# Four PSUM banks as one tile, paired clips and exponentials, and a third set of exponentials added on VectorE

## The chip, the cores and the metric

The kernel runs on one core of a Trainium2 chip. The metric is the device time of one execution in microseconds (us). The times come from repeated runs; the profile is of one further execution, in which the hardware profiler recorded every instruction. In the text PE is TensorE, DVE is VectorE, ACT is ScalarE, POOL is GpSimd and SP is SyncE, which here issues loads.

## The reference, cut to what matters

Eight batches of 112 tokens with 512 channels go through two layers. Each layer is a cross-attention over 375 context rows followed by a feed-forward network, each on a layer-normalised input and added to the residual. The change touches the second cross-attention, which has 16 heads of 32 channels:

```python
scores = jnp.einsum('bhsd,bhtd->bhst', q, k) / scale
scores = jnp.clip(scores, -50.0, 50.0)
scores = jnp.where(attend, scores, -10000.0)
scores = jnp.clip(scores, -50.0, 50.0)
probs = jax.nn.softmax(scores, axis=-1)
ctx = jnp.einsum('bhst,bhtd->bhsd', probs, v)
ctx = ctx.transpose(0, 2, 1, 3).reshape(B, S, H)
delta = rs * (ctx @ Wo.T + bo)
delta = (delta - mu) / jnp.sqrt(var + EPS_LN) * ln_gamma + ln_beta
x = x + delta
```

Since scores are clipped to 50 in size, the kernel takes no maximum: it clips, takes the exponential, and divides the weighted sum of values by the sum of the exponentials.

## The kernel before

The kernel is one long program. Layer 0 (attention, then a feed-forward network with ternary weights) fills the first 206 us of the span; then come the queries of layer 1; then, from 234.6 to 395.6 us, the second attention, called the stage below; then the last feed-forward network.

In the stage the loop runs over batches `b` (0 to 7) and, in each, over three chunks `c` of 125 context rows. The order in which each engine gets its work is the order in which the program writes it: `manual_schedule` covers all five engines here. Each engine works strictly through its own queue, so an instruction that waits holds up everything behind it on that engine.

For each chunk:

- `scores(b, c)`: PE multiplies keys with queries, for 4 groups `dc` of four heads `r` each. The four heads of a group lie on four different row quarters of PE, run side by side, and write four different PSUM banks, one per `r`. Each bank holds 4 x 112 = 448 columns. DVE then clips each bank into SBUF (L910, with `upper` carrying the mask) and ACT takes the exponential in place (L911). The results are `sets[(b + c) % 3][r]`.
- `fill(1)`: one step of a generator that projects keys (L194, four steps per batch) or values (L203, three steps) of a later batch. It keeps PE occupied while DVE and ACT work on the chunk. Its result goes through one of two PSUM buffers called "mm", which ACT copies out (L197 or L205). The table `STEPS` says in how many chunks of a batch a step is taken; batch 4 has two, all the others three.
- `sums` of the chunk before: PE multiplies exponentials with values (`num`, L931). With the last chunk of a batch it also forms the denominator (`den`, L926), by multiplying the exponentials with a block of ones. The exponentials of chunks 0 and 1 have by then been added together by `add(b)` (L897, on POOL in batches 0 to 6, on DVE in batch 7), so `den` takes two passes: the added set, and chunk 2. ACT copies both out (L937, L938).

Beside this each batch carries work for others:

- chunk 0: DVE finishes a transpose of earlier tokens (L848), then `project_end(b - 3)` (L822 to L827), which waits for POOL's `f` and tokens (L815, L816).
- chunk 1: `divide(b - 1)` on DVE: reciprocals of the denominators (L947) and products (L948).
- chunk 2: `write4(b - 3)` on DVE (L837), `project_product(b - 2)` on PE (L803, into an "mm" buffer, from the divided attention), then `project_begin(b - 2)`: DVE adds the bias out of that buffer (L809), takes moments and a scaled difference (L143 to L817), POOL takes an inverse root step by step (L105 to L109) and updates tokens (L816). Then PE transposes what `write4` wrote (L844, into the other "mm" buffer).

In most chunks POOL and ACT also convert integer weights of the last feed-forward network (L880 on ACT, L882 on POOL), out of two buffers `raw` that SP refills by DMA (L869) as soon as L882 has read them. `convert_integers` stands ahead of `scores` in each chunk, `add(b)` ahead of it at chunk 2.

The PSUM tiles named "s" come from the pool `ps_s`, with four buffers of one bank each. The query stage before (L742, L225) and the last feed-forward network (L1039, L1040) take theirs from it too.

Of the kernel before, what the change touches and what calls it, by code (L numbers as in the profile page):

```python
# [23 lines left out]
F32 = mybir.dt.float32  # L24
# [6 lines left out]
ALU = mybir.AluOpType  # L31
AX = mybir.AxisListType
PSUM = bass.MemoryType.PSUM
ENGINES = mybir.EngineType

P = 128
B, T, D = 8, 112, 512
KC = D // P
S2, CK = 375, 125
NCK = S2 // CK  # L40
# [5 lines left out]
NR = P // HD  # L46
# [10 lines left out]
CLIP = 50.0 / SC1  # L57
# [7 lines left out]

SPLIT = 2.0 ** -12
LESS = 1.0 - 2.0 ** -13


@with_exitstack  # L70
def two_layers(ctx: ExitStack, tc: tile.TileContext, x, ctxT, ctxN, mask0, mask1, w1, w2, w3,
               wq, wk, wv, wo, bq, bk, bv, bo, gamma, beta, rscale,
               wg, sg, wu, su, wd, sd, out):
    nc = tc.nc
# [630 lines left out]

    tailp = ctx.enter_context(tc.tile_pool(name="tailp", bufs=1, side="right"))

    ps_s = ctx.enter_context(tc.tile_pool(name="ps_s1", bufs=4, space=PSUM))
    ps_mm = ctx.enter_context(tc.tile_pool(name="ps_mm1", bufs=2, space=PSUM))
    kv_psum[0] = ps_mm  # L710

# [11 lines left out]
    upper = tailp.tile([CK, NCK, B], F32, name="upper")  # L723
# [127 lines left out]
    with tc.tile_pool(name="work2", bufs=1, side="right") as work2, \  # L851
            tc.tile_pool(name="ps_av", bufs=1, space=PSUM) as ps_av, \
            tc.manual_schedule(engines={ENGINES.PE, ENGINES.SP, ENGINES.DVE,
                                        ENGINES.Activation, ENGINES.Pool}):

        todo = [(w, which, half, c, min(PIECE, HALVES[which][half + 1] - c))
                for which, w in enumerate((wg, wu, wd)) for half in range(2)
                for c in range(HALVES[which][half], HALVES[which][half + 1], PIECE)]  # L860
        due = {(0, 1): 2, (0, 2): 2, (1, 0): 1, (1, 1): 2, (1, 2): 2, (2, 0): 1,
               (3, 1): 2, (3, 2): 2, (4, 0): 1, (5, 1): 2, (5, 2): 2, (6, 0): 1,
               (6, 1): 2, (6, 2): 2, (7, 0): 1, (7, 1): 2, (7, 2): 2}
        loaded = []

        def load_integers(count):
            for w, which, half, c, n in todo[:count]:
                raw = work2.tile([P, PIECE], I32, name="raw", bufs=2)[:, :n]
                nc.sync.dma_start(out=raw, in_=w[:, c:c + n])  # L869
                loaded.append((raw, which, half, c - HALVES[which][half], n))  # L870
            del todo[:count]

        def convert_integers():
            for raw, which, half, c, n in loaded:
                if (which, half) not in halves:
                    halves[which, half] = slab("w", F32R)
                t = halves[which, half][:, c:c + n]

                k = pieces.pop()
                nc.scalar.activation(t, raw, AF.Square, bias=zero_point,  # L880
                                     accum_out=squares[:, k:k + 1])
                nc.gpsimd.tensor_scalar(t, raw, -128.0, 1.0, ALU.add, ALU.mult)  # L882
            loaded.clear()

        sets = [[work2.tile([P, KC, T], F32, name=f"e{i}{r}") for r in range(NR)]  # L890
                for i in range(NCK)]

        def add(b):
            add = (nc.gpsimd if b in ADD_POOL else nc.vector).tensor_add
            for r in range(NR):
                e, e1 = (sets[(b + c) % NCK][r][:CK] for c in range(2))
                add(e, e, e1)  # L897

        def scores(b, c):
            kT = kvs_of[b][0]  # L900
            ss = [ps_s.tile([CK, KC, T], F32, name="s") for r in range(NR)]
            for dc in range(KC):
                for r in range(NR):
                    rows = slice(r * HD, (r + 1) * HD)
                    nc.tensor.matmul(ss[r][:, dc, :], lhsT=kT[rows, dc, c * CK:(c + 1) * CK],  # L905
                                     rhs=qT[rows, dc, b * T:(b + 1) * T], start=True, stop=True)
            es = sets[(b + c) % NCK]
            for r in range(NR):
                e = es[r][:CK]
                nc.vector.tensor_scalar(e, ss[r], upper[:, c, b:b + 1], -CLIP, ALU.min, ALU.max)  # L910
                nc.scalar.activation(e, e, AF.Exp, scale=SC1)  # L911
            return es

        def sums(b, c, es):
            if c == 0:
                sums.num = ps_av.tile([P, KC, T], F32, name="num")
            num = sums.num
            v = kvs_of[b][1]  # L920
            if c == NCK - 1:
                den = ps_av.tile([P, KC, T], F32, name="den")
                added = sets[b % NCK]
                for k, of in enumerate((added, es)):
                    for r in range(NR):
                        nc.tensor.matmul(den[r * HD:(r + 1) * HD], lhsT=ones[:CK, :HD],  # L926
                                         rhs=of[r][:CK], start=(k == 0), stop=(k == 1))
            for dc in range(KC):
                for r in range(NR):
                    head = slice((4 * dc + r) * HD, (4 * dc + r + 1) * HD)  # L930
                    nc.tensor.matmul(num[r * HD:(r + 1) * HD, dc, :], lhsT=v[:, c, head],  # L931
                                     rhs=es[r][:CK, dc, :], start=(c == 0 and dc == 0),
                                     stop=(c == NCK - 1 and dc == KC - 1))
            if c == NCK - 1:

                rden = added[0]
                nc.scalar.copy(rden, den)  # L937
                nc.scalar.copy(qT[:, :, b * T:(b + 1) * T], num)  # L938
                rdens[b] = rden

        def divide(b):

            n = (b + 1) * T - (b + 1) * T // P * P
            for t0, t1 in ((0, T - n), (T - n, T)):
                rden, of = rdens[b][:, :, t0:t1], qT[:, :, b * T + t0:b * T + t1]
                if t1 > t0:
                    nc.vector.reciprocal(rden, rden)  # L947
                    nc.vector.tensor_mul(of, of, rden)  # L948


        STEPS = [3, 3, 3, 3, 2, 3, 3, 3]
        ADD_POOL = range(B - 1)
        last, rdens, later = None, {}, []
        folding = fold_bias()
        counts = list(due.values())
        load_integers(counts.pop(0))
        for b in range(B):
            for c in range(NCK):
                if c == 2 and b in ADD_POOL:
                    add(b)  # L960
                if (b, c) in due:
                    convert_integers()
                    if counts:
                        load_integers(counts.pop(0))
                es = scores(b, c)
                if c == 2 and b not in ADD_POOL:
                    add(b)
                if c < STEPS[b]:
                    fill(1)
                if c == NCK - 1:  # L970
                    sums(*last)
                if (b, c) == (B - 1, NCK - 1):
                    over = tailp.tile([P, 29], F32, name="over")
                    nc.gpsimd.tensor_scalar(over, squares, WIDE, 1.0, ALU.is_gt, ALU.mult)
                if b == 0 and c > 0:
                    next(folding)
                if c == 0:
                    while later:
                        later.pop()()
                    if b >= 3:  # L980
                        project_end(b - 3)
                elif c == 1 and b >= 1:
                    divide(b - 1)
                elif c == 2:
                    turned = 3 <= b < 3 + GROUPS[0][1]
                    if turned:
                        write4(b - 3)
                    if b >= 2:
                        project_product(b - 2)
                    if b == B - 1:  # L990

                        hits = ps_s.tile([1, 29], F32, name="s")
                        nc.tensor.matmul(hits, lhsT=ones[:, :1], rhs=over, start=True, stop=True)
                        wide = tailp.tile([1, 1], I32, name="wide")
                        nc.vector.tensor_reduce(wide, hits, AX.X, ALU.max)
                    if b >= 2:
                        project_begin(b - 2)
                    if turned:
                        later.append(transpose4(b - 3, ps_mm, "mm"))
                if last and c < NCK - 1:  # L1000
                    sums(*last)
                last = b, c, es

        nc.scalar.activation(stat.tile([CK, 1], F32, name="peak")[:], es[-1][:CK, 0, :1], AF.Silu)
        sums(*last)
        divide(B - 1)
        project_end(B - 3)
# [197 lines left out]
```

## Time and profile before

| | |
|---|---|
| runs | 516.91, 517.08, 518.55 us; median 517.08 |
| profiled execution | 516.34 us, its span 514.2 us, mean granted PE clock 0.997 |
| second attention stage | 234.6 to 395.6 us of the span |
| PE start of the chunks (b, 0) for b = 4, 5, 6, 7 | 310.77, 329.15, 350.62, 370.95 us |
| clips L910 | 96 of 125 x 448, mean 677 ns |
| exponentials L911 | 96 of 125 x 448, mean 570 ns |
| adds L897 on POOL | 28 of 125 x 448, mean 1213 ns |
| denominators L926 | 128 rows of 125 x 448 columns, 16 per batch, in some 1.5 us |

The span runs from the first to the last instruction; the time of an execution has some 2 us around it. In timeline rows the columns are the start, the duration of the merged rows, engine, line, operation, output and inputs with their shapes, the number of instructions, and in brackets how long the engine stood idle before and what released it. A float32 matrix product shows as two rows, so the 8 products of a denominator show as 16 rows. Rows that follow each other on one engine overlap a little; the distance from start to start tells what one costs in a series.

### The profile page before, as it was taken

How to read it: one execution, taken by the hardware profiler on the slowest of the kernel's cores; microseconds unless marked ns; L12 is line 12 of the kernel's file. 1: busy time of each engine (PE TensorE's matmuls, PEld its weight loads, DVE VectorE, ACT ScalarE, POOL GpSimd, SP SyncE). 2: the span in 40 equal slices, each digit the busy share in tenths (PEclk: the TensorE clock that was granted, in tenths of full speed). 3: DMA queues.
4: the chain of work that ended last, by engine and by line, in shares of the span. 5: the costliest groups of instructions: out<-in, count | busy, mean ns of one | idle time of the engine just before them, and what ended most of it. 6: DMA issues, size and time to landing. Idle time of an engine off the chain costs nothing.

```text
span 514.2 us, 8868 instructions
## 1 busy us (share of the span) xinstructions
PE 502.5 (98%) x3402; PEld 315.8 (61%) x3402; DVE 337.2 (66%) x815; ACT 252.8 (49%) x438; POOL 134.4 (26%) x221
## 2 busy tenths in 40 slices
PE   9999999999999999999999999999999999999995
PEld 6445554455545455696565565555555788889984
DVE  3552548767798987965676688986897753334432
ACT  0326656857565666236675366465665233103310
POOL 0000121110111064211551475674754430000000
PEclk9999999999999999999999999999999999999998
DMA  8998795200120100122421112012320000010001
GB/s 241 347 407 326 268 324 205 80 18 0 61 82 1 60 2 0 45 101 61 162 68 51 62 52 62 3 53 62 98 69 13 20 1 1 20 42 20 1 20 48
DMA packets 13489, 45.77 MB, mean 89 GB/s; under 512 B 2097, under 2 KB 3392, under 8 KB 12288
## 3 DMA queue, kind: packets, MB, share of 16 engines
q1 hardware_dynamic: 11888, 41.43, 23.5%
q0 software_dynamic: 1248, 3.70, 2.2%
q8 instruction: 29, 0.48, 0.4%
q14 instruction: 20, 0.16, 0.1%
q10 hardware_dynamic: 304, 0.01, 0.0%
HBM read 41.46 MB, written 1.84 MB: 84 GB/s over the span
## 4 chain that ended last, share of the span: by engine, by line
PE 47%; DVE 6%; POOL 2%; ACT 1%; DMA 1%; issue 1%; DVEq 0%; POOLq 0%; ACTq 0%
PE s L1045 14%; PE mm L203 8%; PE down L1067 7%; PE mm L803 3%; PE s L905 3%; PE num L931 2%; PE mm L194 2%; DVE e L910 2%; PE den L926 2%; PE mm L740 1%; PE mm L738 1%; DMA raw<-in_wd_dram 1%; PE s L744 1%; DVE e L947 1%; ACT e L911 1%
## 5 line engine op out<-in xcount | busy, mean ns | idle before, releaser
L203 PE MATMUL mm<-wv,cT 128*125 128x512 f32 x192 | 87.6, 599 | 0.0
L194 PE MATMUL mm<-cT,wk 128*128 128x375 f32 x256 | 87.3, 485 | 0.0
L1045 PE MATMUL s<-h4T,w 128*128 128x512 f32 (+1 forms) x352 | 72.6, 367 | 0.2 <-PE num L931 0.2
L1045 PEld LDWEIGHTS s<-h4T,w 128*128 128x128 f32 x352 | 63.5, 188 | 8.8 <-PE num L931 0.4
L910 DVE TENSOR_SCALAR e<-s,upper 125x448 f32<-125x448 f32 x96 | 59.0, 677 | 14.7 <-PE s L905 13.9
L911 ACT ACTIVATE e<-e 125x448 f32<-125x448 f32 x96 | 51.6, 570 | 27.8 <-DVE e L910 27.3
L194 PEld LDWEIGHTS mm<-cT,wk 128*128 128x128 f32 x256 | 46.8, 190 | 27.6 <-issue 1.0
L203 PEld LDWEIGHTS mm<-wv,cT 128*125 128x125 f32 x192 | 34.5, 187 | 38.0 <-issue 36.4
L897 POOL TENSOR_TENSOR e<-e,e 125x448 f32<-125x448 f32 x28 | 33.1, 1213 | 15.8 <-PE num L931 15.8
L1067 PE MATMUL down<-w,gu 128*128 128x512 f32 (+1 forms) x176 | 37.0, 367 | 0.0
L541 PE MATMUL mm<-w_q,q_qT 128*128 128x512 fp8e4 (+1 forms) x168 | 34.8, 361 | 0.8 <-DVE tokens L583 0.4
L439 POOL DMA_DIRECT2D tokens<-x x14 | 10.7, 768 | 90.3 <-DVE x L433 63.0
L1067 PEld LDWEIGHTS down<-w,gu 128*128 128x128 f32 x176 | 29.8, 188 | 5.7
L880 ACT ACTIVATE w<-raw,zero_point 128x640 fp32r<-128x640 int32 (+2 forms) x29 | 22.6, 781 | 20.4 <-DMA raw<-in_wd_dram 9.2
L1053 ACT CAST gu<-gu 128x512 fp32r<-128x512 f32 (+1 forms) x22 | 12.5, 568 | 39.6 <-DVE gu L1051 39.6
L570 POOL TENSOR_SCALAR q<-gu 128x704 bf16<-128x704 f32 x14 | 10.8, 790 | 79.8 <-ACT gu L567 79.8
L882 POOL TENSOR_SCALAR w<-raw 128x640 fp32r<-128x640 int32 (+2 forms) x29 | 20.7, 724 | 36.0 <-ACT w L880 35.8
L905 PE MATMUL s<-qT,kv 32*125 32x112 f32 x768 | 29.4, 280 | 0.6 <-DVE qT L748 0.3
L1051 DVE SCALAR_TENSOR_TENSOR gu<-s,su,gu 128x512 f32<-128x512 f32 (+1 forms) x22 | 15.1, 684 | 21.8 <-PE s L1045 20.6
L905 PEld LDWEIGHTS s<-qT,kv 32*125 32x125 f32 x768 | 24.5, 183 | 7.1 <-issue 5.8
L541 PEld LDWEIGHTS <-q_qT 128*128 128x128 bf16 x168 | 16.3, 98 | 19.7 <-issue 2.5
L931 PEld LDWEIGHTS num<-e,kv 125*32 125x32 f32 x768 | 18.4, 110 | 13.6 <-issue 7.9
(238 smaller groups left out, 798.6 us busy)
## 6 DMA issues: line engine op xcount, KB each, us to landing
cT<-in_ctxT_dram SPq DMA_DIRECT2D x13, 750.0 KB, 6.1
raw<-in_w_dram SPq DMA_DIRECT2D x6, 1408.0 KB, 20.3
cN<-in_ctxN_dram SPq DMA_DIRECT2D x8, 768.0 KB, 4.5
raw<-in_wg_dram SPq DMA_DIRECT2D x8, 320.0 KB, 3.0
raw<-in_wu_dram SPq DMA_DIRECT2D x8, 320.0 KB, 2.9
raw<-in_wd_dram SPq DMA_DIRECT2D x8, 320.0 KB, 3.1
out_dram<-d SPq DMA_DIRECT2D x6, 256.0 KB, 2.0
wk<-in_wk_dram SPq DMA_DIRECT2D x4, 256.0 KB, 4.9
```

The source lines that it names most:

```text
L194: nc.tensor.matmul(ps[dc], lhsT=wk_s[:, kc, dc * P:(dc + 1) * P], rhs=cT[:, kc, :], start=(kc == 0), stop=(kc == KC - 1))
L203: nc.tensor.matmul(ps, lhsT=cT[:, kc, c * CK:(c + 1) * CK], rhs=wv_s[:, kc, :], start=(kc == 0), stop=(kc == KC - 1))
L541: nc.tensor.matmul(ps[:, :n], lhsT=qT[:, kc, :], rhs=w[:, kc * H + n0:kc * H + n0 + n], start=(kc == 0), stop=(kc == KC - 1))
L880: nc.scalar.activation(t, raw, AF.Square, bias=zero_point, accum_out=squares[:, k:k + 1])
L882: nc.gpsimd.tensor_scalar(t, raw, -128.0, 1.0, ALU.add, ALU.mult)
L897: add(e, e, e1)
L905: nc.tensor.matmul(ss[r][:, dc, :], lhsT=kT[rows, dc, c * CK:(c + 1) * CK], rhs=qT[rows, dc, b * T:(b + 1) * T], start=True, stop=True)
L910: nc.vector.tensor_scalar(e, ss[r], upper[:, c, b:b + 1], -CLIP, ALU.min, ALU.max)
L911: nc.scalar.activation(e, e, AF.Exp, scale=SC1)
L931: nc.tensor.matmul(num[r * HD:(r + 1) * HD, dc, :], lhsT=v[:, c, head], rhs=es[r][:CK, dc, :], start=(c == 0 and dc == 0), stop=(c == NCK ...
L1045: nc.tensor.matmul(ps[:, :n], lhsT=w[:, c:c + P], rhs=h4T[k][:, kc, :n], start=(kc == 0 and k == 0), stop=(kc == KC - 1 and k == 1))
L1067: nc.tensor.matmul(ps, lhsT=gus[k][:, hc, j * P:(j + 1) * P], rhs=w[:, c + n0:c + n0 + n], start=(hc == 0 and k == 0), stop=(hc == HC - 1 ...
```

## The change

Three things change.

The pool `ps_s` gets a single tile of four banks, and a small class `Banks` hands out parts of it: `tile` gives the next bank, in rotation, and `pair` gives two neighbouring banks, starting at an even one.

In the stage, `scores` takes two pairs in place of four tiles. Heads 0 and 1 are in the first pair and heads 2 and 3 in the second. One clip and one exponential then treat 2 x 448 elements per partition. The exponentials lie in tiles for two heads (`twos`); `add(b)` adds two heads' groups at a time.

In batches 2 to 6 (`ADD_LAST`), DVE adds the exponentials of chunk 2 to the sum that POOL has made of chunks 0 and 1. The two adds stand in chunk 2 behind `write4` and `project_product` and ahead of `project_begin`. The denominator of these batches is then one pass over the sum.

```diff
+class Banks:
+    def __init__(self, pool):
+        self.all = pool.tile([P, 4, 512], F32, name="s")
+        self.next = 0
+    def tile(self, shape, dtype, name):
+        n = 1
+        for d in shape[1:]:
+            n *= d
+        t = self.all[:shape[0], self.next, :n]
+        self.next = (self.next + 1) % 4
+        return t if len(shape) == 2 else t.rearrange("p (a b) -> p a b", a=shape[1])
+    def pair(self):
+        k = (self.next + 1) // 2 * 2 % 4
+        self.next = (k + 2) % 4
+        return self.all[:, k:k + 2, :]
...
-    ps_s = ctx.enter_context(tc.tile_pool(name="ps_s1", bufs=4, space=PSUM))
+    ps_s = Banks(ctx.enter_context(tc.tile_pool(name="ps_s1", bufs=1, space=PSUM)))
...
-        sets = [[work2.tile([P, KC, T], F32, name=f"e{i}{r}") for r in range(NR)]
+        twos = [[work2.tile([P, 2, KC, T], F32, name=f"e{i}{h}") for h in range(NR // 2)]
                 for i in range(NCK)]
+        sets = [[two[r // 2][:, r % 2] for r in range(NR)] for two in twos]
...
-            for r in range(NR):
-                e, e1 = (sets[(b + c) % NCK][r][:CK] for c in range(2))
+            for h in range(NR // 2):
+                e, e1 = (twos[(b + c) % NCK][h][:CK] for c in range(2))
                 add(e, e, e1)
+        def add_last(b):
+            for h in range(NR // 2):
+                e, e1 = (twos[(b + c) % NCK][h][:CK] for c in (0, NCK - 1))
+                nc.vector.tensor_add(e, e, e1)
...
-            ss = [ps_s.tile([CK, KC, T], F32, name="s") for r in range(NR)]
+            ss = [ps_s.pair() for h in range(NR // 2)]
...
-                    nc.tensor.matmul(ss[r][:, dc, :], lhsT=kT[rows, dc, c * CK:(c + 1) * CK],
+                    nc.tensor.matmul(ss[r // 2][:CK, r % 2, dc * T:(dc + 1) * T], lhsT=kT[rows, dc, c * CK:(c + 1) * CK],
...
-            for r in range(NR):
-                e = es[r][:CK]
-                nc.vector.tensor_scalar(e, ss[r], upper[:, c, b:b + 1], -CLIP, ALU.min, ALU.max)
+            for h in range(NR // 2):
+                e = twos[(b + c) % NCK][h][:CK].rearrange("p a k t -> p a (k t)")
+                nc.vector.tensor_scalar(e, ss[h][:CK, :, :KC * T], upper[:, c, b:b + 1], -CLIP,
+                                        ALU.min, ALU.max)
                 nc.scalar.activation(e, e, AF.Exp, scale=SC1)
...
-                for k, of in enumerate((added, es)):
+                parts = (added,) if b in ADD_LAST else (added, es)
+                for k, of in enumerate(parts):
                     for r in range(NR):
                         nc.tensor.matmul(den[r * HD:(r + 1) * HD], lhsT=ones[:CK, :HD],
-                                         rhs=of[r][:CK], start=(k == 0), stop=(k == 1))
+                                         rhs=of[r][:CK], start=(k == 0),
+                                         stop=(k == len(parts) - 1))
...
+        ADD_LAST = range(2, B - 1)
...
+                    if b in ADD_LAST:
+                        add_last(b)
                     if b >= 2:
                         project_begin(b - 2)
```

## The prediction

> **What bounds the kernel now.** I read the page's busy table and clock row first, then TensorE's (PE's) timeline through the second attention stage (234.6 to 395.6 us of the span), then VectorE's (DVE's) and GpSimd's (POOL's) beside it, then single groups.
>
> ```profile
> span 514.2 us, 8868 instructions
> PE 502.5 (98%) x3402; PEld 315.8 (61%) x3402; DVE 337.2 (66%) x815; ACT 252.8 (49%) x438; POOL 134.4 (26%) x221
> PEclk9999999999999999999999999999999999999998
> L910 DVE TENSOR_SCALAR e<-s,upper 125x448 f32<-125x448 f32 x96 | 59.0, 677 | 14.7 <-PE s L905 13.9
> L911 ACT ACTIVATE e<-e 125x448 f32<-125x448 f32 x96 | 51.6, 570 | 27.8 <-DVE e L910 27.3
> ```
>
> PE is busy 98% at the full clock: over the whole kernel it is the bound, and only work taken from PE, or a stall of it, moves the end. Clips (L910) and exponentials (L911) run beside it.
>
> ```profile
> 300.70 1.80 PE L905 MATMUL s<-qT,kv 32*125 32x112 f32 x32
> 314.57 1.71 PE L926 MATMUL den<-e,ones 125*32 125x448 f32 x16
> 316.09 0.95 PE L931 MATMUL num<-e,kv 125*32 125x112 f32 x32
> 328.59 0.63 PE L844 MATMUL mm<-ident,d 128*128 128x128 f32 x4 [0.34 <-ACT e L911]
> ```
>
> PE's timeline of the stage. A score group takes 1.14 us elsewhere; at 300.70 it takes 1.80, because its fourth bank was still being clipped (clips end 301.33). So 98% hides places where DVE is already the last to come. A denominator's 16 rows take 316.09 - 314.57 = 1.52 us of PE.
>
> ```profile
> 309.80 0.69 DVE L809 TENSOR_TENSOR d<-mm,bo 128x512 f32<-128x512 f32 x1 [0.28 <-PE mm L803]
> 316.57 0.88 DVE L822 SCALAR_TENSOR_TENSOR tokens<-d,ln_f,tokens 128x512 f32<-128x512 f32 x1 [0.88 <-POOL tokens L816]
> 318.88 2.45 DVE L910 TENSOR_SCALAR e<-s,upper 125x448 f32<-125x448 f32 x4
> 325.53 2.46 DVE L910 TENSOR_SCALAR e<-s,upper 125x448 f32<-125x448 f32 x4
> 328.36 0.68 DVE L809 TENSOR_TENSOR d<-mm,bo 128x512 f32<-128x512 f32 x1
> 350.29 0.69 DVE L809 TENSOR_TENSOR d<-mm,bo 128x512 f32<-128x512 f32 x1 [2.73 <-PE mm L803]
> 370.29 0.69 DVE L809 TENSOR_TENSOR d<-mm,bo 128x512 f32<-128x512 f32 x1 [1.23 <-PE mm L803]
> ```
>
> DVE's timeline, L809 (start of `project_begin`) in batches 3, 4, 5 and 6. From 309.80 to 328.36 DVE and POOL form a closed ring of 18.56 us: L809 to L817, POOL's root and L816 (311.77 to 316.53), `project_end` (316.57 to 318.88), clips of chunk 1, `divide` (321.25 to 325.43), clips of chunk 2, `write4`, next L809. Nothing in it waits for PE but the first row's 0.28. PE's own batch 4 (310.77 to 329.15) is 18.38 us: both are equally long. Batches 5 and 6 are longer on PE (21.47 and 20.33), so there DVE waits for the product, 2.73 and 1.23. In batch 2 that wait is 3.94.
>
> **The change part by part.**
> *Denominators.* Batches 2 to 6 lose 8 of 16 rows: 1.52/2 = 0.76 us each, 3.8 us of PE in all.
>
> *Paired clips.* Four clips take 2.46 us, one 0.677, so they start (2.46 - 0.677)/3 = 0.594 apart: 448/0.96 = 467 ns of elements at one per cycle of 0.96 GHz (the clock in the Trainium skill, "VectorE: DVE Perf Modes", errata section) and 127 fixed. Two of 896 elements start 0.933 + 0.127 = 1.06 apart: 2.12 for 2.37 from start to next work, 0.25 less per chunk. The bounds are 0 (if crossing a bank cost the 127 again) and 0.25; I take 0.25.
>
> *Paired exponentials.* 1.96 for four, 0.576 for one: 0.46 apart, of which 0.09 fixed. Two take about 1.79. ACT is idle before L911 for 27.8 us, so that is off the path, except where a conversion (L880) comes ahead. The last exponential then ends about 0.1 later after the last clip, under PE's fill (2.7 to 3.6 us) or, in batch 4's chunk 2, its product; without that cover it would cost 0.1 in each of 24 chunks, 2.4 us.
>
> *POOL's add* (L897), 4.7 us for four, becomes two, estimated 4.4 to 4.8. It gives way to nothing critical: in batch 4 it ends at 327.52, exponentials at 328.60. Behind it on POOL are the weight conversions (L882), behind those SP's loads (L869), which wait for L882's buffers, and ACT's L880 for those. The change issues no new DMA. DVE's own add in batch 7 becomes 2.0 for 2.13, ahead of a wait of 2.57 for PE: nothing.
>
> *Banks as one tile.* Same rotation of four banks; heads keep separate banks, the score group already needed all four free. Cost 0 if waits are kept per bank; the rivals price it if not.
>
> *Added adds.* DVE, batches 2 to 6, after `write4` and before `project_begin`. The row is L897 in batch 7:
>
> ```profile
> 388.35 2.22 DVE L897 TENSOR_TENSOR e<-e,e 125x448 f32<-125x448 f32 x4
> 389.38 1.78 POOL L882 TENSOR_SCALAR w<-raw 128x640 fp32r<-128x640 int32 x1 [1.78 <-ACT w L880]
> 341.64 0.43 DVE L948 TENSOR_TENSOR qT<-qT,e 128x256 f32<-128x256 f32 x1
> 343.36 1.14 DVE L948 TENSOR_TENSOR qT<-qT,e 128x192 f32<-128x192 f32 x1
> ```
>
> Four start (2.22 - 0.62)/3 = 0.533 apart, 66 ns fixed; two of 896 take 2 x (0.933 + 0.066) = 2.0 us. Each waits for its pair's exponential on ACT and for POOL's add, and everything behind it on DVE waits too: L809, with it the release of the product's bank (one of two "mm" banks, which the next batch's fill needs), POOL's root, and the next clips.
>
> The rows also show what a neighbour on POOL does: 192 elements took 1.14 us while POOL added, 256 took 0.43 with POOL still; in batch 7 it was POOL that stretched, 0.72 to 1.78. The Trainium skill ("SBUF — State Buffer", Who interferes with whom) says that a DVE instruction with two SBUF inputs contends with a POOL instruction that reads SBUF, and that the later one waits. That speaks against this change: by the free row the adds cost 2.0 us, by the rule up to one or two conversions (0.72 each) more where L882 follows POOL's add, in batches 3, 5 and 6. In batch 3 POOL's pieces would run until about 308.9 and the adds begin at 308.5. I take 0.2 us per such batch, and keep 0 and 0.7 as ends.
>
> **The sum, by L809's start.**
> - Until batch 2: PE waited 0.8 us at 267 for clips (1,2), behind `divide(0)`; two groups of clips are 0.5 shorter: -0.5. The adds of batch 2 lie in the wait of 3.94.
> - Batch 3: clips (3,1) start at 298.87 - 0.5 = 298.4, end 0.25 sooner again; so scores (3,2) come 0.76 early, but the 0.76 saved at den(2) is spent waiting for these clips. `divide(2)` ends at 305.7, clips (3,2) 307.9, `write4` 308.4, adds 310.4. L809 at 310.4 for 309.80: +0.6.
> - Batch 4: ring 18.56 - 0.5 + 2.0 = 20.06: 330.5 for 328.36, +2.15. The fill of (5,0) needs its bank at 331.2, PE is there about 330.3: a stall near 0.9.
> - Batch 5: DVE had `write4` done at 347.57 and waited. Now 347.57 + 2.15 - 0.5 = 349.2; the exponentials, behind ACT's conversions that follow the ring, give the first add 349.6; L809 at 351.6 for 350.29: +1.3.
> - Batch 6: likewise first add 370.25, L809 at 372.25 for 370.29: +1.96. The transposes wait for ACT's copy behind the exponentials (+1.2), so scores (7,0) come at about 372.2 for 370.95. The fill behind them needs the product's bank at 373.0 and is there at 373.2: 0.2 to spare.
> - Batch 7 is PE's again (DVE's last waits are for PE), with den(6) shorter: +1.2 - 0.76 = +0.4. POOL's port in three batches: +0.6.
> In all +1.0 us: the ring takes back the whole 3.8. The feed-forward after it keeps its length: product 6 starts at 403.3 and `divide(7)` ended at 400.5, so 2.9 us of lateness there are covered.
> The profiled execution took 516.34 (span 514.2 and 2.14 around it), so 517.3; the median of the three runs is 517.08, 0.74 above it, so 518.1.
>
> **The rivals.**
> 1. *The adds fit.* DVE waits for the product in batches 2, 3, 5 and 6 (3.94, 0.28, 2.73, 1.23), which at first sight pays for adds of 2.0 less 0.75 of clips per batch. If ring and exponentials are less late than I have them, PE keeps 1.6 to 5 us of 3.8 + 1.5 (the pairs' own gain, by the stalls at 267, 300, 328 and 361): 512 to 515.5, about 514.3. For it: batch 5's room. Against: den's saving brings the product forward by just what it saves, and the wait shrinks with it.
> 2. *Adds held at the shared port* (slower). Place: batches 3, 5, 6, adds against L882. At one conversion per add, +0.7 to 1.4 in each. It decides from 0.2 us on, because the fill of (7,0) then stands still and each further 0.1 is 0.1 of the end: 520 to 522.
> 3. *The tile is guarded as a whole.* Scores would hardly notice. But in the last feed-forward, gate and up groups would wait for each other's Silu and multiply (0.69 + 0.68 us, 22 pairs): +30 us, 547. Nothing in this trace shows it; every bank was its own tile.
>
> **How the numbers follow.** Ring closed: 0.58, from -1.0 to +2.8 (516.1 to 519.9; ends from clips 0 to 0.25, adds 2.0 to 2.3, landing of loads, where two rows differ by a microsecond). A measurement of this kernel tells 0.3%, 1.55 us, from no change: of this case 0.32 lies within, 0.26 above. Rival 1: 0.22 (0.20 beyond 0.3%, 0.02 within). Rival 2: 0.17 (0.16 and 0.01). Rival 3: 0.03. So faster 0.20, same 0.35, slower 0.45. The range goes down to 514.3, the middle of rival 1, and up to 522.0, the end of rival 2.
>
> **What would show it.** Right: den rows in batches 2 to 6 near 0.8 us; L910 x48 near 1.14 us; L809 starts about 20 us apart from batch 3 to 4 and later than before by 1 to 2 in batches 4 to 6; PE fill stalled once after batch 4; scores (3,2) and (6,2) waiting longer than before. Wrong: L809 still waiting for PE in batches 5 and 6 (rival 1); adds over 1.3 us each (rival 2); Silu and multiply between every gate pair (rival 3); a fixed cost in paired clips.

## The result, and the profile after

The changed kernel took 565.05 us (median of 4 runs, 564.80 to 567.18) where the kernel before took 517.0: a ratio of 1.0935, 95% interval 1.0898 to 1.0971. The forecast was 518.1 with a range up to 522.0, so it was wrong by 47 us.

Line numbers move with the edit: the gate and up products L1045 are L1079 after, Silu L1050 is L1084, the multiplication behind it L1051 is L1085, clips L910 are L938, exponentials L911 are L940, POOL's adds L897 are L921, `project_begin`'s bias add L809 is L831, the division's products L948 are L979. The page of after, first its span and engines, then groups (after the bars: busy time and mean ns of one; idle time ahead of them and what ended most of it):

```profile
span 562.9 us, 8638 instructions
PE 506.1 (90%) x3362; PEld 313.7 (56%) x3362; DVE 346.3 (62%) x775; ACT 245.9 (44%) x390; POOL 130.8 (23%) x207
...
L1079 PE MATMUL s<-h4T,w 128*128 128x512 f32 (+1 forms) x352 | 80.7, 383 | 34.1 <-DVE gu L1085 34.0
...
L940 ACT ACTIVATE e<-e 125x896 f32<-125x896 f32 x48 | 44.8, 946 | 42.3 <-DVE e L938 40.6
L938 DVE TENSOR_SCALAR e<-s,upper 125x896 f32<-125x896 f32 x48 | 53.0, 1145 | 15.6 <-PE s L934 14.9
```

The same products on the page of before:

```profile
L1045 PE MATMUL s<-h4T,w 128*128 128x512 f32 (+1 forms) x352 | 72.6, 367 | 0.2 <-PE num L931 0.2
```

PE stood idle for 0.2 us ahead of these products before, and for 34.1 after, nearly all of it until DVE's multiplication L1085 had ended. That is the last feed-forward network, a stage whose code the diff does not touch: it only takes its "s" tiles from the object that the diff replaced. In each of its groups PE forms two products, called gate and up, each in its own bank; ACT takes Silu of the gate, and DVE multiplies the result with the up product. The timeline of after in that stage (start, duration, engine, line; in brackets the idle time ahead and what ended it):

```profile
411.71 5.41 PE L1079 MATMUL s<-h4T,w 128*128 128x512 f32 x16 [5.08 <-DVE gu L1085]
...
439.33 0.69 ACT L1084 ACTIVATE gu<-s,sg 128x512 f32<-128x512 f32 x1 [3.50 <-PE s L1079]
440.05 0.75 DVE L1085 SCALAR_TENSOR_TENSOR gu<-s,su,gu 128x512 f32<-128x512 f32 x1 [3.50 <-ACT gu L1084]
...
440.86 4.00 PE L1079 MATMUL s<-h4T,w 128*128 128x512 f32 x16 [1.62 <-DVE gu L1085]
...
446.48 4.00 PE L1079 MATMUL s<-h4T,w 128*128 128x512 f32 x16 [1.62 <-DVE gu L1085]
```

And of before:

```profile
424.78 11.60 PE L1045 MATMUL s<-h4T,w 128*128 128x512 f32 x49
...
427.37 0.69 ACT L1050 ACTIVATE gu<-s,sg 128x512 f32<-128x512 f32 x1 [0.45 <-PE s L1045]
429.25 0.75 DVE L1051 SCALAR_TENSOR_TENSOR gu<-s,su,gu 128x512 f32<-128x512 f32 x1 [1.60 <-PE s L1045]
...
431.11 0.69 ACT L1050 ACTIVATE gu<-s,sg 128x512 f32<-128x512 f32 x1 [0.45 <-PE s L1045]
```

Read the order. Before, PE runs without a gap, Silu starts while the up product is still going, and a group of gate and up (16 matmuls) takes 431.11 - 427.37 = 3.74 us. After, Silu starts only when both products are done, the multiplication follows, and only then does PE start the next group, in other banks: 446.48 - 440.86 = 5.62 us. The difference, 1.88 us, is the wait of 1.62 and 0.26 in which each group now ends before anything follows it.

Not every group loses the same. The 11 groups of 512 columns lose 25.6 us, and the first four of them some 14 of that: their multiplications stand on DVE behind the last division and projection (the first waits for a load too), so PE waits 5.08 us for the first (the row at 411.71) and 3.78 for the third. Behind these two long waits the products themselves were slower as well, 5.41 and 5.54 us for 16 where they take 4.00 later, at a granted PE clock of 0.72 and 0.70; behind the waits of 1.62 it was 1.00, as in all of this stage before until its last 10 us. The 11 groups of 384 columns lose 16.5 us.

The whole difference of the spans, 48.7 us, splits at two rows: the row of the first scores that has waited for the last queries, and the count of hits (L993, L1025 after), a small product in the attention's last chunk.

| part of the span, us | before | after | difference |
|---|---|---|---|
| to scores (0,0) | 235.41 | 239.19 | +3.8 |
| attention | 157.49 | 160.83 | +3.3 |
| from the count to the end | 121.3 | 162.9 | +41.6 |

The query stage shows the same thing. Its transposes L249 write "s" tiles too, and in the timeline of after they stand behind readers of the tile before:

```profile
220.26 0.66 PE L249 MATMUL s<-ident,d 128*128 128x128 f32 x4 [0.85 <-DVE qT L770]
222.33 0.66 PE L249 MATMUL s<-ident,d 128*128 128x128 f32 x4 [1.41 <-DVE h2T L255]
...
226.62 0.66 PE L249 MATMUL s<-ident,d 128*128 128x128 f32 x4 [0.85 <-DVE qT L770]
```

These three waits make 3.1 of the 3.8 us; the trace of before has none of the three.

### The profile page after: what moved, and what is told of

The parts are those of the page before. It is cut to its first block, busy times and chain, and to the rows that moved or that the text cites. A ratio compares the mean times of both kernels' runs of the same rounds, so it can differ in the third digit from the quotient of the medians.

```text
span 562.9 us, 8638 instructions
## 1 busy us (share of the span) xinstructions
PE 506.1 (90%) x3362; PEld 313.7 (56%) x3362; DVE 346.3 (62%) x775; ACT 245.9 (44%) x390; POOL 130.8 (23%) x207
## 4 chain that ended last, share of the span: by engine, by line
PE 37%; DVE 18%; POOL 3%; issue 2%; ACT 2%; DMA 1%; DVEq 0%; ACTq 0%; POOLq 0%; SPq 0%
PE s L1079 13%; PE down L1101 6%; PE mm L225 6%; DVE e L938 4%; DVE e L978 3%; DVE gu L1085 2%; PE s L934 2%; DVE qT L979 2%; ACT gu L1084 2%; PE mm L825 2%; PE num L962 1%; POOL ln_t L130 1%; PE mm L762 1%; PE mm L760 1%; PE s L766 1%
## 5 line engine op out<-in xcount | busy, mean ns | idle before, releaser
L1079 PE MATMUL s<-h4T,w 128*128 128x512 f32 (+1 forms) x352 | 80.7, 383 | 34.1 <-DVE gu L1085 34.0
L1079 PEld LDWEIGHTS s<-h4T,w 128*128 128x128 f32 x352 | 64.6, 194 | 49.7 <-DVE gu L1085 41.1
L940 ACT ACTIVATE e<-e 125x896 f32<-125x896 f32 x48 | 44.8, 946 | 42.3 <-DVE e L938 40.6
L938 DVE TENSOR_SCALAR e<-s,upper 125x896 f32<-125x896 f32 x48 | 53.0, 1145 | 15.6 <-PE s L934 14.9
L1085 DVE SCALAR_TENSOR_TENSOR gu<-s,su,gu 128x512 f32<-128x512 f32 (+1 forms) x22 | 15.0, 684 | 63.8 <-ACT gu L1084 62.6
L1084 ACT ACTIVATE gu<-s,sg 128x512 f32<-128x512 f32 (+1 forms) x22 | 13.9, 634 | 78.0 <-PE s L1079 73.3
L921 POOL TENSOR_TENSOR e<-e,e 125x896 f32<-125x896 f32 x14 | 30.8, 2221 | 13.4 <-PE num L962 11.6
L934 PE MATMUL s<-qT,kv 32*125 32x112 f32 x768 | 27.4, 279 | 4.0 <-DVE e L938 3.3
L934 PEld LDWEIGHTS s<-qT,kv 32*125 32x125 f32 x768 | 23.1, 183 | 10.3 <-DVE e L938 4.8
L825 PE MATMUL mm<-wo,qT 128*128 128x512 f32 x56 | 25.8, 603 | 0.6 <-DVE qT L979 0.6
```

The source lines that it names most:

```text
L825: nc.tensor.matmul(ps, lhsT=qT[:, kc, i * P:(i + 1) * P], rhs=wo_s[:, kc, :], start=(kc == 0), stop=(kc == KC - 1))
L934: nc.tensor.matmul(ss[r // 2][:CK, r % 2, dc * T:(dc + 1) * T], lhsT=kT[rows, dc, c * CK:(c + 1) * CK], rhs=qT[rows, dc, b * T:(b + 1) * T ...
L938: nc.vector.tensor_scalar(e, ss[h][:CK, :, :KC * T], upper[:, c, b:b + 1], -CLIP, ALU.min, ALU.max)
L1079: nc.tensor.matmul(ps[:, :n], lhsT=w[:, c:c + P], rhs=h4T[k][:, kc, :n], start=(kc == 0 and k == 0), stop=(kc == KC - 1 and k == 1))
L1084: nc.scalar.activation(gu[:, :n], gate[:, :n], AF.Silu, scale=sg_s[:, hc:hc + 1])
L1085: nc.vector.scalar_tensor_tensor(gu[:, :n], up[:, :n], su_s[:, hc:hc + 1], gu[:, :n], ALU.mult, ALU.mult)
```

## The experiments

**The tile: where it is used, and how it is cut.** Theory A is that waits follow the tile and not the bank: a write into any bank of a lasting tile waits for every reader of the tile, a read for every writer. Its rivals put the time into the attention, or into something else in the change.

`e1_stage_only`: after, but the lasting tile serves the attention alone; the query stage and the last feed-forward network take one-bank buffers as before.

```diff
-    ps_s = Banks(ctx.enter_context(tc.tile_pool(name="ps_s1", bufs=1, space=PSUM)))
...
+    ps_stage = ctx.enter_context(ExitStack())
+    ps_s = ps_stage.enter_context(tc.tile_pool(name="ps_s1", bufs=4, space=PSUM))
...
+    ps_stage.close()
+    ps_s = Banks(ps_stage.enter_context(tc.tile_pool(name="ps_s2", bufs=1, space=PSUM)))
...
+    ps_stage.close()
+    ps_s = ps_stage.enter_context(tc.tile_pool(name="ps_s3", bufs=4, space=PSUM))
```

The second pool is opened ahead of the attention, the third ahead of the feed-forward network.

> The changed kernel, with the lasting tile kept for the second attention alone: the query stage and the last feed-forward take their 's' tiles from pools of four one-bank buffers again. Theory A (the tile is guarded as a whole, so a matmul into one bank waits for the readers of another): the feed-forward's 41.7 us and the query stage's 3.8 us go, the attention's own 3.2 us stay: 565.05 - 45.5 = 519.5 us. Rival B (pairing the instructions, or the adds, is what slowed the kernel, in the attention and by what it leaves behind): nothing goes, 565. Rival C (only the strict rotation of banks matters): as A, the two are told apart by the two-tile kernels.

`e2_tile_alone`: before, with nothing of the change but the lasting tile (the class `Banks` comes with it).

```diff
-    ps_s = ctx.enter_context(tc.tile_pool(name="ps_s1", bufs=4, space=PSUM))
+    ps_s = Banks(ctx.enter_context(tc.tile_pool(name="ps_s1", bufs=1, space=PSUM)))
```

> The kernel before, with nothing changed but the pool: one lasting tile of four banks, handed out bank by bank. Clips, exponentials, adds and denominators as before. Theory A: query stage +3.8, feed-forward +41.7, attention 0 to 1, since the score groups waited for all four banks already: 517.0 + 45.5 to 46.5, about 563 us. Rival B (the paired instructions or the adds): 517.

`e3a_two_tiles_aligned`: after, with two lasting tiles of two banks; gate and up of a group lie in one of them. `tile` and `pair` hand out banks of these two.

```diff
-        self.all = pool.tile([P, 4, 512], F32, name="s")
+        self.two = [pool.tile([P, 2, 512], F32, name=f"s{h}") for h in range(2)]
...
-                gate = ps_s.tile([P, 512], F32, name="s")
-                up = ps_s.tile([P, 512], F32, name="s")
+                both = ps_s.pair()
+                gate, up = both[:, 0, :], both[:, 1, :]
```

> The changed kernel with two lasting tiles of two banks in place of one of four; in the last feed-forward gate and up of a group take the two banks of one tile, so that the next group has the other tile. Theory A: the Silu still waits for the up product, but the next group's matmuls no longer wait for this group's multiply: the feed-forward comes back to about 119 us, the query stage keeps 1 to 3 us of its 3.8, the attention its 3.2: 521 to 523 us. Rival C (the strict rotation of four banks): as slow as the changed kernel, 565.

`e3b_two_tiles_crossed`: the same two tiles, but gate and up take the next bank in turn, as in after.

> As the aligned one, but gate and up keep the bank that is next: behind the one bank that the check for wide weights takes, gate lies in the second bank of one tile and up in the first bank of the other. Same tiles, same number of banks, only which share a tile differs. Theory A: the next gate shares its tile with this up, so it waits for this group's multiply, but the Silu need not wait for up any more: a stall of about 0.95 us per group where it was 1.62, some 22 groups: 22 to 28 us above the aligned kernel, about 547. Rival C: 565 as the changed kernel; if only the number of banks per tile mattered, as the aligned kernel.

| kernel | us | ratio to before, 95% interval | from the count to the end |
|---|---|---|---|
| after | 565.05 | 1.0935 [1.0898, 1.0971] | 162.9 |
| e2_tile_alone | 564.10 | 1.0913 [1.0891, 1.0936] | 165.2 |
| e1_stage_only | 521.14 | 1.0088 [1.0067, 1.0109] | 121.3 |
| e3a_two_tiles_aligned | 524.00 | 1.0149 [1.0126, 1.0173] | 122.3 |
| e3b_two_tiles_crossed | 540.07 | 1.0454 [1.0431, 1.0476] | 137.6 |

The tile alone (e2) makes the kernel as slow as after, and taking it out of the two other stages (e1) takes 43.9 of the 48.05 us away. (The feed-forward network of e2 is 2.3 us longer than that of after: behind its two long waits the granted clock was 0.54 and 0.58, and 16 products took 6.77 and 6.48 us.) The waits from 395 us on, summed (engine and line, what it waited for, us in total, times, longest), for e2_tile_alone:

```profile
ACT gu L1072 <- PE s L1067: 75.6, 21, 7.3
...
PE s L1067 <- DVE gu L1073: 33.9, 19, 5.0
```

for e3a_two_tiles_aligned, where PE's wait for DVE is gone but for one of 1.25 us, and Silu's for the up product in the same tile has stayed:

```profile
ACT gu L1081 <- PE s L1076: 31.2, 19, 7.3
```

and for e1_stage_only and before, where it is the multiplication that waits for the up product:

```profile
DVE gu L1090 <- PE s L1084: 20.7, 17, 1.6
```

```profile
DVE gu L1051 <- PE s L1045: 20.6, 17, 1.6
```

So the engines and the number of banks are the same in all of these, and the waits change with the bounds of the tile: rival B (something else in the change) and rival C (the strict rotation of banks) are out. With two banks to a tile, the group that PE writes and the group that is read lie in different tiles, and PE runs on; Silu still waits for the up product, 1.6 us on average, which costs next to nothing because PE hardly ever waits for it: from the count to the end e3a takes 122.3 us, before 121.3.

e3b came out 16 us above e3a where 22 to 28 were expected. Its timeline shows why, with both cases in one run:

```profile
429.59 4.00 PE L1076 MATMUL s<-h4T,w 128*128 128x512 f32 x16 [0.91 <-DVE gu L1082]
434.50 3.99 PE L1076 MATMUL s<-h4T,w 128*128 128x512 f32 x16 [0.91 <-DVE gu L1082]
...
485.05 30.69 PE L1076 MATMUL s<-h4T,w 128*128 128x384 f32 x176
```

For the first 512 tokens the gate lies in one tile and the up product in the other, and nearly every group waits, most of them 0.91 us and not 1.62, since Silu no longer waits for the up product and only the multiplication is left in the gap. Then three transposes (L863) take one bank each, the rotation is three banks further, and for the last 384 tokens gate and up fall into one tile by chance: 176 matmuls without a gap. That the same line stalls or runs by the parity of its bank is the plainest sign that the tile is what the program guards.

Two more totals came above what was expected: e1 took 521.1 us for 519.5, because its first scores still come 2.5 us later than before, and e3a 524.0 for 521 to 523.

**What is left of the change without the tile.** e1 is 1.0088 of before, more than the sum allowed. Its attention takes 160.56 us against 157.49, so the tile elsewhere hid a second, smaller error. Four runs take the rest apart. Three of them have the tile in the attention and one-bank buffers elsewhere, like e1; the fourth, f4, has no such tile. (In e1 and the three the first scores come 1.2 to 2.5 us later than before, although the query stage has one-bank buffers: 0.89 us of PE "issue" at its start and a wait of 0.72 for the last queries in place of 0.31. Closing and reopening the buffers may do that; it was not tried alone. The attention's own length leaves it out.)

`f1_no_last_adds`: e1 with `ADD_LAST = ()`, so no added adds.

> The stage-only kernel (521.1 us) without DVE's adds in batches 2 to 6: all denominators take two passes again; clips, exponentials and POOL's adds stay paired. Theory R (the ring of DVE and POOL is the bound in batches 3 to 6, the adds lengthen it by 2.0 us each, POOL's longer adds lengthen the divisions): 2.0 us less for the end, 519.1; the start of project_begin 4 comes about 18.9 us after that of project_begin 3 in place of 20.8. Rival P (the paired instructions are what costs, the adds fit in waits): PE gets 3.8 us of denominators back, so about 525.

`f2_pool_adds_single`: e1 with POOL's adds as four of 448 columns again.

```diff
-            for h in range(NR // 2):
-                e, e1 = (twos[(b + c) % NCK][h][:CK] for c in range(2))
+            for r in range(NR):
+                e, e1 = (sets[(b + c) % NCK][r][:CK] for c in range(2))
                 add(e, e, e1)
```

> The stage-only kernel (521.1 us) with POOL's add as four instructions of 448 elements, as before the change; all else paired, DVE's adds in batches 2 to 6 stay. Theory L (a multiplication of the division that meets POOL's add waits for the instruction that POOL has begun, 2.2 us where it was 1.1): in batches 4 to 6 the divisions' multiplications come back from 1.8, 3.2 and 3.2 us to 1.0, 1.6 and 1.1, and the end comes 2.2 us sooner, about 518.9. If the length of POOL's instructions does not matter: 521.1, multiplications as they were.

`g4_pairs_alone`: both of these edits, so paired clips and exponentials alone.

> The kernel after with one-bank buffers outside the attention (as in e1_stage_only), POOL's adds again four of 448, and no added adds: what is left of the change is the paired clips and exponentials on a lasting tile. Theory A (they save 0.25 us of DVE per chunk, and DVE closes the steps of the ring in batches 2 to 6, so part of it comes through; the later query stage of the earlier runs with this edit, 1.2 us, stays): the attention takes 156.2 to 156.8 us against 157.49, the whole 516.4 to 517.2. Rival (a clip of 1.15 us keeps two banks where two of 0.59 us gave the first back early, and PE's next scores wait longer than DVE saves): attention 158 us or more, 518 to 519.

`f4_adds_without_pairs`: before, with the added adds of batches 2 to 6 (four of 448) and the denominator in one pass.

> The kernel before (516.7 us), its pools and its one-bank tiles, with DVE's adds in batches 2 to 6 alone, as four of 448 each, and one-pass denominators there. Theory R: the ring is 18.56 + 2.13, so the end is 2.3 us later, about 519.1, although PE has 3.8 us less to do. If the adds fit in the waits for the product (the first rival of the prediction): up to 3.8 us faster, 513.

The attention, from scores (0,0) to the count, and the ratio of the whole:

| | no added adds | added adds in batches 2 to 6 |
|---|---|---|
| pairs, POOL adds four of 448 | g4: 157.15 us, 1.0008 [1.0001, 1.0014] | f2: 159.13, 1.0038 [1.0024, 1.0052] |
| pairs, POOL adds two of 896 | f1: 159.34, 1.0058 [1.0036, 1.0079] | e1: 160.56, 1.0088 [1.0067, 1.0109] |
| no pairs | before: 157.49 | f4: 162.24, 1.0100 [1.0081, 1.0120] |

Each length is of one profiled execution; the feed-forward network, which these kernels share, differs by up to 0.6 us between them, so differences of half a microsecond say nothing. Read so: the added adds cost 2.0 us with POOL's short adds and 1.2 with its long ones; the long adds cost 2.2 us without the added ones and 1.4 with them. The ratios of all runs give 1.5 us for the added adds and 2.6 for the long ones in either case, each uncertain by 1 to 1.5 us. So each costs something; whether one makes the other cheaper is not shown. Pairing alone (g4) changes nothing that can be told: 0.3 us less in the attention, where 0.7 to 1.3 was expected, and a total 0.08% above before, its later first scores included. Where the added adds have made DVE the one that closes the ring, pairing gives 3.1 us (f4 to f2; f2 also pairs the added adds and has the tile in the attention).

Two expectations of ring steps failed, and for one reason. f4 took 521.5 us for 519.1: its step from `project_begin` of batch 3 to that of batch 4 was 21.50 us, 2.94 above before, of which the adds are 2.13; the other 0.8 is a multiplication of 192 columns in `divide`, 0.36 us before and 1.19 here. f1 took 519.2 us as expected, but that is in part luck, since its step was 19.66 us for 18.9; there the same multiplication took 2.12.

Why that multiplication grows, and why a longer add on POOL costs anything, is seen on DVE. In before it began just ahead of POOL's adds:

```profile
322.69 0.36 DVE L948 TENSOR_TENSOR qT<-qT,e 128x192 f32<-128x192 f32 x1
322.78 4.74 POOL L897 TENSOR_TENSOR e<-e,e 125x448 f32<-125x448 f32 x4 [1.30 <-PE num L931]
```

The timeline of g4_pairs_alone at batch 4, POOL's adds and the multiplications of `divide`:

```profile
323.03 4.71 POOL L924 TENSOR_TENSOR e<-e,e 125x448 f32<-125x448 f32 x4 [0.67 <-PE num L965]
323.33 1.05 DVE L982 TENSOR_TENSOR qT<-qT,e 128x192 f32<-128x192 f32 x1
...
326.08 0.67 DVE L982 TENSOR_TENSOR qT<-qT,e 128x256 f32<-128x256 f32 x1
```

and of f1_no_last_adds, which differs in the form of POOL's adds only:

```profile
322.95 4.24 POOL L924 TENSOR_TENSOR e<-e,e 125x896 f32<-125x896 f32 x2 [0.78 <-PE num L965]
323.14 2.12 DVE L982 TENSOR_TENSOR qT<-qT,e 128x192 f32<-128x192 f32 x1
...
326.95 0.52 DVE L982 TENSOR_TENSOR qT<-qT,e 128x256 f32<-128x256 f32 x1
```

POOL's work became shorter, 4.24 for 4.71, and DVE's longer, 2.12 for 1.05. The multiplication begins just behind the start of POOL's first add and ends 0.1 to 0.2 us after that add has ended: at 324.38 where an add takes about 1.2 us, at 325.26 where it takes 2.1. So the price is not the bytes but what is left of the one POOL instruction that is running. In the same two kernels the two multiplications of the division beside POOL's add of batch 6 take 2.01 + 1.20 us with long adds against 1.06 + 0.29. The two divisions together are 2.8 us longer, which is enough for the 2.2 to 2.6 that long adds cost.

**Where the adds do pay.** In batches 0 and 1 no projection stands behind the adds; DVE waits for PE there.

`f5_adds_in_batches_0_1`: f4 with `ADD_LAST = (0, 1)`. `g1_adds_in_0_1_6`: with `(0, 1, 6)`. `g3_pairs_and_adds_0_1`: g4 with `(0, 1)`.

> As the one before, but with DVE's adds and one-pass denominators in batches 0 and 1, where project_begin and project_end do not run yet and DVE waits for PE. Theory R: the adds are covered and PE keeps both savings of 0.76: 1.5 us faster than before, about 515.2. If each add holds the clips behind it and PE with them: 517 or more.

> The kernel before with the added adds in batches 0, 1 and 6 alone. Theory A (a step of the ring gains one denominator pass of 0.77 us on PE wherever the adds have room on DVE, which is where PE and not DVE closed the step before: batches 0 and 1, and batch 6, after which no ring of clips follows): one more pass is saved than with batches 0 and 1 alone (514.91), so 514.2, and from the first scores to the count of hits 155.4 us. Rival: the adds of batch 6 push the division and the clips behind them on DVE, and the saved pass comes back as a wait of PE for the count or for batch 7's exponentials: 515 to 516.

> As g4_pairs_alone, with the added adds in batches 0 and 1, where DVE has room. Theory A (the two gains add: 0.77 us of denominators for each of the two batches, and the pairs): 1.5 us below g4_pairs_alone, attention 154.7 to 155.3, the whole 514.9 to 515.7, so no better than the adds alone, since the query stage gives 1.2 us back. Rival (the adds of two heads' groups, 2.1 us, make the clips behind them late): at or above g4_pairs_alone.

| kernel | us | ratio, 95% interval | attention |
|---|---|---|---|
| f5_adds_in_batches_0_1 | 514.91 | 0.9964 [0.9952, 0.9977] | 156.13 |
| g1_adds_in_0_1_6 | 514.21 | 0.9956 [0.9942, 0.9969] | 155.71 |
| g3_pairs_and_adds_0_1 | 515.21 | 0.9975 [0.9965, 0.9985] | 155.50 |

The timeline of f5 shows the adds and the two denominators:

```profile
252.21 2.22 DVE L902 TENSOR_TENSOR e<-e,e 125x448 f32<-125x448 f32 x4
267.04 2.90 DVE L902 TENSOR_TENSOR e<-e,e 125x448 f32<-125x448 f32 x4
```

```profile
255.29 0.96 PE L932 MATMUL den<-e,ones 125*32 125x448 f32 x8
...
271.86 0.96 PE L932 MATMUL den<-e,ones 125*32 125x448 f32 x8
```

Here the adds, 2.2 and 2.9 us, fall into DVE's idle time: its waits for PE ahead of the clips of chunk 1 of the next batch shrink from 3.74 us in before to 1.30 (batch 1), and from 4.83 to 2.36 (batch 2). Of the 1.5 us that two passes are worth the attention keeps 1.4. All three totals came as expected. The pairs add to the gain in g3 (its attention is the shortest), and its later first scores give it back. g1 is the best kernel of the study, 0.44% below before; whether its third batch adds anything to f5 can't be told, since the intervals overlap.

## Why the prediction was wrong, point by point

**Banks as one tile: the step that failed.** "Cost 0 if waits are kept per bank." They were not; they were kept per tile, and the sentence left the other case to rival 3, at a chance of 0.03. Rival 3 has the right place, the right two instructions and the right sequence. The argument against it was that nothing in the trace showed it. But that trace could not have shown it: there every bank was a tile of its own, so the absence of such waits was no evidence on a tile of four banks. The step was an unknown with a far end of +30 us, and it was entered at its near end with the weight of an oddity.

**Rival 3's price** was also low, 30 us for 41.6 in the feed-forward network and 3.1 more by waits in the query stage. The sum 22 x (0.69 + 0.68) took the two instructions alone, 1.37 us per group. An undisturbed group of 512 columns adds 1.88 us: the wait of 1.62 has Silu, the multiplication (0.75 in the timeline) and 0.18 of handing over, and 0.26 more is the end of each group, which the next one used to cover. A group of 384 adds 1.50. The first four add some 3.6 each, for what DVE has to do first and for the lower clock behind the long waits. The query stage has no place in the sum, although the pool that the diff replaced serves it too.

"Scores would hardly notice" held: with the tile alone (e2), the attention took 157.98 for 157.49.

**POOL's add: the second, smaller step that failed.** "It gives way to nothing critical" looked at what stands behind the add on POOL and on its queues. What the longer instruction delays stands on DVE, and a row that the prediction shows has it: 1.14 us for 192 elements beside POOL's adds of about 1.1. The Trainium skill's rule that the prediction cites ("SBUF — State Buffer", Who interferes with whom: the later of the two waits) was weighed for the added adds only, not for the divisions, which meet the same POOL work with longer instructions. The traces agree with the rule: 1.05 us beside the short adds, 2.12 beside the long ones. The prediction put this delay at nothing; it comes to 1.4 to 2.6 us.

**Denominators, clips, exponentials, added adds: right.** In after, the denominator of a batch with added adds and the adds of batch 4 on DVE:

```profile
317.55 0.96 PE L956 MATMUL den<-e,ones 125*32 125x448 f32 x8
...
332.88 2.09 DVE L926 TENSOR_TENSOR e<-e,e 125x896 f32<-125x896 f32 x2
```

Eight rows, and the products behind them start 0.77 us later, for 0.76. The adds take 2.09 us for the 2.0 worked out (2.59 in batch 3). Two clips take 2.21 us in the timelines, four took 2.46: 0.25 saved, as predicted; 448 further columns cost 1145 - 677 = 468 ns, for the 467 that the prediction worked with, so crossing a bank cost nothing. For an exponential they cost 946 - 570 = 376 ns, so of 0.46 us from start to start some 0.09 is fixed, as the prediction had it. None of rival 2's long holds of the adds came: the 2.59 is the worst.

**The sum by L809's start: right in the ring, short by what POOL's adds delay.** The starts of the same add (now L831) in batches 3 to 6 of after:

```profile
314.09 0.68 DVE L831 TENSOR_TENSOR d<-mm,bo 128x512 f32<-128x512 f32 x1
334.88 0.68 DVE L831 TENSOR_TENSOR d<-mm,bo 128x512 f32<-128x512 f32 x1
356.94 0.68 DVE L831 TENSOR_TENSOR d<-mm,bo 128x512 f32<-128x512 f32 x1
379.12 0.68 DVE L831 TENSOR_TENSOR d<-mm,bo 128x512 f32<-128x512 f32 x1
```

None of them waits for PE any more: DVE closes the ring, as the likeliest case had it, and rival 1 ("the adds fit") is out. Less the 3.8 us of the later start they stand at 310.3, 331.1, 353.2 and 375.3, where 310.4, 330.5, 351.6 and 372.25 were predicted: 0.1 early, then 0.6, 1.6 and 3.1 late, growing in the batches whose divisions meet POOL. The ring itself, 20.06 us by the prediction, took 334.88 - 314.09 = 20.79, and 0.77 us of that is the growth of the two multiplications of its division (1.29 + 0.52 for 0.36 + 0.68). In f2, with POOL's short adds, where they take 0.36 + 0.67, the ring took 20.04:

```profile
312.03 0.68 DVE L834 TENSOR_TENSOR d<-mm,bo 128x512 f32<-128x512 f32 x1
332.07 0.68 DVE L834 TENSOR_TENSOR d<-mm,bo 128x512 f32<-128x512 f32 x1
```

The stall of PE's fill behind batch 4 came as well, 0.81 us for about 0.9:

```profile
335.62 3.70 PE L225 MATMUL mm<-wv,cT 128*125 128x512 f32 x8 [0.81 <-DVE d L831]
```

In f2 the attention is 1.6 us longer than before, against +1.0 predicted; the 0.6 that is left is not settled. Without the tile in the other stages the change still loses 3.1 us in the attention, 0.6% and not 0.2%.

**Where the adds were put.** The prediction saw that in batches 2 to 6 the ring takes back what the denominators save. f4 and f5 bear it out from both sides: five added adds where DVE closes the ring made the kernel 1.00% slower, two where DVE was idle made it 0.36% faster. What batch 6 does alone stays open (g1).

## What to carry to other kernels

When a diff turns buffers into slices of one tile, ask first what the program guards, the slice or the tile, and go through every stage that takes buffers from that pool, also those without a changed line; a wait that the old form could not have is not made unlikely by its absence from the old trace. Here two banks that are written and read together could be one tile for 1 us in a stage of 121 (e3a); the whole rotation as one tile cost 41.6. A long stall can cost more than its length: behind waits of 3.8 and 5.1 us PE's granted clock was lower. Work for an engine pays in the steps in which that engine waits, so place it by the idle time ahead of each step and not by a range of loop indices.

## What the runs showed of the hardware

A multiplication of two SBUF operands on DVE that met an add on POOL ended 0.1 to 0.5 us after that POOL instruction, with 128 to 448 columns, in all the traces above (a merged row of POOL taken as equal parts): 192 columns took 0.36 us where they began just ahead of POOL's adds (before, batch 4), 1.05 beside POOL adds of 448 columns, 2.12 beside adds of 896. Merging POOL's instructions shortened POOL's work by a tenth (4.71 to 4.24 us) and doubled the longest delay on DVE. How long one instruction is, and not only how long the work is, is thus a cost to the neighbour.

The granted PE clock followed PE's idle time: in the last feed-forward network of after it was 0.72 and 0.70 in the groups behind waits of 5.08 and 3.78 us, and 1.00 in those behind waits of 1.62. What sets it is not shown.
